# Preparing the first half of a recurrence inside a linear attention, moving the last scatters, and joining PSUM banks of two heads

## Chip, cores, metric

One core of a Trainium2 chip runs one program that computes eight layers, one after the other. The metric is device microseconds from start to end of one execution. Before the change the median of three runs is 2433.83 us (2418.57 to 2437.38).

## What is computed

The input is 4 batches of 1024 tokens with 128 features. Each of eight blocks is `x = layernorm(x + f(x))`. The first four (a gated recurrence, slots, a sparse attention, a two-way mixture) are not touched. What matters here are the blocks five to eight:

```python
# 5: linear attention, 16 heads of 64, causal, cos and sin weighted
S_cos += kc[:, None] * v[None, :];  S_sin += ks[:, None] * v[None, :]
num = qc @ S_cos + qs @ S_sin;  den = max(qc . z_cos + qs . z_sin, 1e-6)
out = (num / den) @ Wo + bo
# 6: eight experts, the two likeliest per token, silu(gate) * up
# 7: recurrence of 16 states for each of 256 channels
x  = resid * rsqrt(mean(resid^2) + eps) * norm_w
xs = silu(conv4(x @ in_w.T));  delta = softplus(xs @ wd1.T @ wd2.T + b)
h  = exp(delta * A) * h + (delta * xs) * B[t];  y = sum_n h_n * C[t]
y  = (y + xs * W_D) * silu(x @ skip_w.T) @ out_w.T;  return resid + y
# 8: eight experts, those within a probability mass of 0.8 per token
```

## The kernel before

Features are kept twice: `xN[b]` with tokens on the partitions and `xT[b]` with features on them, one pair per batch.

**Linear attention** (`l2_attn`, line 919 on). A quarter is 256 tokens of a batch (16 quarters), and a unit is a pair of heads in a quarter: 128 units. The loop over `t` runs a software pipeline: projection of unit `t + 2`, keys of `t + 1`, sums within the quarter (`l2_within`, line 1104) and from the states before (`l2_before`) of unit `t` into the PSUM tiles `po0` and `po1`, one bank for each head; scores and state sums of `t + 1`; then `l2_out` (line 1134) takes unit `t` out of PSUM. TensorE's order in this loop is as written (`manual_schedule`); the other engines are ordered by a scheduler at build time. `l2_out` issues four pairs: ScalarE scales 65 columns into `nsin` (L1142), VectorE multiplies 65 others and adds (`num`, L1145). PSUM is cut into two banks `pj` for projections, values and transposes, `po0`, `po1`, `pr`, and three shared with the experts.

Side work advances by one `yield` per unit: values of the next quarter (`l2_values`, line 1014: a tile `cv1` with a column of ones set by GpSimd at L1019, VectorE's add L1029, ScalarE's scaling L1036; two buffers), the output projection of a quarter, and, after the last quarter of a batch, `l2_dispatch` (line 1271). It ranks the eight experts for each token and scatters the batch's rows into `xrows` by 16 indirect DMAs on GpSimd (L1359), each made to wait for a recent projection (`beat`) so that they are spread out. As soon as the rows of a batch are there, the experts of block 6 (`l2_ffn`, line 1377, 23 units of 128 rows per batch) advance by one step per unit. A step loads the weights of one expert (`wx`, 384 KB on SP's queue, four buffers), and runs an expert unit on TensorE. `l2_combine` gathers a batch's results by 16 indirect DMAs on GpSimd (L1504), weighs and adds them and normalizes; it is a side generator that advances once per step. After it the batch is `done`.

**Recurrence** (`l3`, line 1549). It works in eight halves, 512 tokens each, two per batch. `l3_prepare` (line 1652) makes what a half needs: norm, transposes, projection `pxe`, a convolution of four taps on VectorE, tanh, the projections `pdb` and `pd`, softplus out of Abs, Exp and Ln, and the tiles `dl` (delta), `ud` (delta times input) and `rows` (B and C, stored to DRAM on SP's queue). `l3_scan` (line 1752) does 16 steps: SP loads a row of B and of C to all partitions (`bn`, `cn`, 256 KB each, four buffers), GpSimd multiplies `db = ud * bn` (L1782), ScalarE takes the exponential `da` (L1786), VectorE scans (L1787), GpSimd multiplies `hc = db * cn` (L1798), and TensorE adds up the 16 results in PSUM (`pys`). For the last three batches pairs of `hc` are added by a DMA first (L1802). Beside the scan of one half the next half is prepared, the one before is finished, the remaining steps of block 6 run (two per scan step in the first half, one in the others) and the experts of block 8 (`l3_experts`, `ph` and `py` with weights `wh`) take three or four steps per scan step. What is left of them runs after the last scan.

Before the first scan, `l3` runs block 6 until batch 0 is `done`, and then prepares half 0 with a step of block 6 at each `yield`. Since tile pools of the recurrence (`l3_pools`, line 1641) take the place of those of the linear attention, this starts when the linear attention ends.

Of the kernel before, what the change touches and what calls it, by code (L numbers as in the profile page):

```python
# [18 lines left out]
P = 128  # L19
# [39 lines left out]
class Net:  # L59
# [859 lines left out]
    def l2_attn(self, load, dispatch, moe):  # L919
# [7 lines left out]
        with ExitStack() as ctx:  # L927
# [9 lines left out]
            for t, n in dict(pj=2, po0=1, po1=1, pr=1).items():  # L937
                self.psq[t] = ctx.enter_context(
                    tc.tile_pool(name=f"ps_{t}", bufs=n, space=bass.MemoryType.PSUM)
                )  # L940
# [12 lines left out]
            side = []  # L953
# [9 lines left out]
            for t in range(-2, n + 4):  # L963
# [20 lines left out]
                if "put" in self.m2["st"][0] if t > 0 else False:  # L984
                    early(moe)
                if 0 <= t < n:
                    self.l2_out(units[t])
                    if t % NP2 == NP2 - 1:
                        Q = units[t]["Q"]
                        side.append(self.l2_project_out(Q))  # L990
                        if Q["c0"] + NQ == NC:
                            side[-1] = chain(side[-1], dispatch(Q["b"]))
# [3 lines left out]
            for g in side:  # L996
                for f in g:
                    pass
# [15 lines left out]
    def l2_values(self, Q):  # L1014
        nc, c2 = self.nc, self.c2
        wp = c2["wp"]
        for c in range(2):
            v1 = wp.tile([P, NH2, VW], F32, name="cv1")
# [85 lines left out]
    def l2_within(self, u):  # L1104
        Q, hp = u["Q"], u["hp"]
        u["po"] = [self.psb(f"po{i}", [P, 2, 2 * VW], f"po{i}") for i in range(2)]
        for i in range(2):
            for c in range(2):
                self.nc.tensor.matmul(  # L1109
                    out=u["po"][i][:, c, :],  # L1110
                    lhsT=u["a"][:, i, c, :],
                    rhs=Q["v"][c][:, 2 * hp + i, :, :].rearrange("p a d -> p (a d)"),
                    start=c == 0,
                    stop=False,
                    skip_group_check=True,
                )

    def l2_before(self, u):

        Q, hp = u["Q"], u["hp"]  # L1120
        for c in range(1 if Q["q"] == 0 else 0, 2):
            s = slice(c * P, (c + 1) * P)
            for i in range(2):
                h = self.HALF[i]
                self.nc.tensor.matmul(
                    out=u["po"][i][:, c, :],
# [7 lines left out]
    def l2_out(self, u):  # L1134
# [3 lines left out]
        for i in range(2):  # L1138
            for c in range(2):
                k = Q["c0"] + c  # L1140
                t = wp.tile([P, VW], F32, name="nsin", bufs=4)
                nc.scalar.activation(  # L1142
                    t, po[i][:, c, VW : 2 * VW], AF.Copy, scale=trig[:, k, 1:2]
                )
                nc.vector.scalar_tensor_tensor(  # L1145
                    num[:, c, i, :], po[i][:, c, 0:VW], trig[:, k, 0:1], t, ALU.mult, ALU.add
                )
# [123 lines left out]
    def l2_dispatch(self, b):  # L1271
# [84 lines left out]
        key, put = f"put{b}", []  # L1356
        for c in range(NC):
            for k in range(2):
# [10 lines left out]
                self.tc.add_to_no_dep_group(key, i)  # L1369

                self.tc.add_manual_dep(i, self.beat.name, SYNC, reason="spread out")
# [5 lines left out]
    def l2_ffn(self, wp):  # L1377
# [10 lines left out]
        for t in range(-8, n + 4):  # L1388
# [18 lines left out]
            for g in side[:]:  # L1407
                if next(g, self) is self:
                    side.remove(g)
# [124 lines left out]
    def l3_load(self):  # L1534
        return dict(
            wskip=self.load("s_in", [P, 2, E3]),
            we=self.load("s_e", [P, 2, ND + D]),
            wd2=self.load("s_d2", [DDELTA + 1, E3]),
            br=self.load_row("h_br", NE),
            wr=self.load("h_router", [P, NE]),  # L1540
            b2=self.load("h_b2", [NE, D]),
        )

    def load_row(self, name, n):
        t = self.const.tile([P, n], F32, name=f"sb_{name}")
        self.nc.sync.dma_start(out=t, in_=self.io[name].to_broadcast([P, n]))
        return t

    def l3(self, w3, moe, fp):

        nc, tc, c = self.nc, self.tc, self.const
# [8 lines left out]
        c3 = self.c3  # L1563
        neg1 = c.tile([P, 1], F32, name="neg1")
        nc.vector.memset(neg1, -1.0)
        c3.update(w3, aneg=aneg, cw=cw, neg1=neg1)
# [3 lines left out]
        while "done" not in self.m2["st"][0]:  # L1570
            next(moe)
        for f in self.l3_prepare(halves[0]):
            next(moe)
        work = self.l3_experts(fp)
        c3["todo"] = []
        end = iter(())
        for i, u in enumerate(halves):
# [6 lines left out]
            for f in self.l3_scan(u):  # L1584
                next(end, None)
                next(nxt, None)
                busy = next(moe, moe) is not moe
# [53 lines left out]
    def l3_pools(self, ctx):  # L1641
# [3 lines left out]
        dp = ctx.enter_context(  # L1645
            tc.tile_pool(name="ssmd", bufs=2, space=bass.MemoryType.DRAM)
        )
        banks = ctx.enter_context(self.banks(y0=1, y1=1, da=2, ff=4))
        self.mtags = dict(t="ff", h=("ff",), o="ff")
        self.c3 = dict(sp=sp, wp=wp, dp=dp, ctx=ctx, banks=banks)  # L1650

    def l3_prepare(self, u):

        nc, c3, b, h = self.nc, self.c3, u["b"], u["h"]
        sp, wp, dp = c3["sp"], c3["wp"], c3["dp"]
        wdb = c3["we"][:, :, 0:ND]

        sq = sp.tile([P, 4, D], F32, name="sq3", tag="s1")
        ms = wp.tile([P, 4], F32, name="ms3")
# [12 lines left out]
        pt = self.psb("ff", [P, 4, P], "pt")  # L1672
        for k in range(4):
            self.tr(pt[:, k, :], sq[:, k, :])
        xnT = wp.tile([P, 512], F32, name="xnT")
# [6 lines left out]
        tail = wp.tile([P, 2, K1], F32, name="tail") if h == 0 else u["prev"]["tail"]  # L1682
        u["tail"] = tail
        xs = wp.tile([P, 2, 512], F32, name="xs3")
        for ec in range(2):
            p = self.psb("ff", [P, 512], "pxe")
            self.mm(p, c3["wskip"][:, 1, ec * P : (ec + 1) * P], xnT)
            xc = sp.tile([P, 512], F32, name="xc", tag="s1")
# [28 lines left out]
        db = sp.tile([ND, 512], F32, name="db1", tag="s2")  # L1717
        rows = dp.tile([2 * NST, 512], F32, name="rows")
        p = self.psb("ff", [ND, 512], "pdb")
# [6 lines left out]
        dl = wp.tile([P, 2, 512], F32, name="dl")  # L1726
        ud = wp.tile([P, 2, 512], F32, name="ud")
        us = sp.tile([P, 2, 512], F32, name="sp_u")
        v = sp.tile([P, 2, 512], F32, name="sp_w")
        p2 = []  # L1730
        for ec in range(2):
            p2.append(self.psb("ff", [P, 512], f"pd{ec}"))
            self.mm(p2[ec], c3["wd2"][:, ec * P : (ec + 1) * P], db[0 : DDELTA + 1, :])
            nc.scalar.activation(us[:, ec, :], p2[ec], AF.Abs)
            nc.vector.tensor_single_scalar(dl[:, ec, :], p2[ec], 0.0, ALU.max)
        nc.scalar.activation(us, us, AF.Exp, scale=-1.0)
        nc.scalar.activation(v, us, AF.Identity, bias=self.ones[:, 0:1])

        for ec in range(2):
            nc.scalar.activation(p2[ec], v[:, ec, :], AF.Identity, bias=c3["neg1"])  # L1740
        nc.scalar.activation(v, v, AF.Ln)
        yield
        for ec in range(2):
            p = p2[ec]
            nc.vector.tensor_sub(p, us[:, ec, :], p)
            nc.vector.tensor_add(p, dl[:, ec, :], p)
            nc.vector.tensor_add(p, v[:, ec, :], p)
            nc.vector.tensor_mul(ud[:, ec, :], xs[:, ec, :], p)
            nc.scalar.copy(dl[:, ec, :], p)  # L1749
# [338 lines left out]
def program(tc, io):  # L2088
    with ExitStack() as ctx:
# [7 lines left out]
        )  # L2097
        with ExitStack() as ff:
            last = n.front(ff, w0, W, d, dp)
            keep = ctx.enter_context(tc.tile_pool(name="moek", bufs=1, side="right"))  # L2100
            mt = ctx.enter_context(tc.tile_pool(name="moet", bufs=2, side="right"))
# [4 lines left out]
        later = {}  # L2106

        def load():
            n.l2_ffn_load()
            later.update(n.l3_load())  # L2110
            n.l2_rows(keep, md, dp)

        moe = n.l2_ffn(mt)
        with w2:
            md = w2.enter_context(tc.tile_pool(name="moed", bufs=1, side="right"))
            n.l2_attn(load, n.l2_dispatch, moe)
        n.l3_pools(ctx)
        fp = ctx.enter_context(tc.tile_pool(name="top", bufs=2, side="right"))
        n.l3(later, moe, fp)
# [17 lines left out]
```

## Time and profile before

| What | us |
|---|---|
| median of 3 runs | 2433.83 |
| profiled execution | 2426.07 |
| its span, first to last instruction | 2424.3 |
| TensorE busy | 2077.0 (86%) |
| VectorE, ScalarE busy | 1439.7, 1335.6 |
| GpSimd busy | 860.8 |
| first and last `pqk` projection of the linear attention | 638.0, 1376.7 |
| last copy of attention output (`coT`) | 1399.3 |
| first and last `db` on GpSimd | 1476.8, 2261.4 |
| last `pys` | 2283.2 |
| end of last `h_acc` | 2416.9 |

Busy times are of one execution on the one core. TensorE's overlapping passes make its busy time an upper view of its work. A share over the whole span mixes stages with different limits, so the stages are read one by one. A line number is one of the kernel before; L127 is the helper that issues matmuls, so that those are told apart by the names of their tiles.

### The profile page before, as it was taken

Reading aid. Unit: us, or ns where it says so; the run is one execution under the profiler, and the core shown is the slowest. Engines: PE = TensorE matmul, PEld = TensorE weight load, DVE = VectorE, ACT = ScalarE, POOL = GpSimd, SP = SyncE. Lnnn points to the kernel's source line nnn. Section 1 sums busy time; section 2 is a strip of 40 time slices with the busy share of each in tenths; the row PEclk is TensorE's granted clock in tenths of the full one; section 3 lists DMA queues with packets and bytes.
Section 4 is the critical chain, followed back from the end, with each engine's and each line's share of the span. In section 5 each row is a group of like instructions: output and inputs, shape, how many; then the busy total and the mean of one; then the engine's idle time right before and its main releaser. Section 6 shows DMA issues by size and latency. Waiting matters only on the chain. (4 is left out here: it accounts for less than half of the span.)

```text
span 2424.3 us, 35395 instructions
## 1 busy us (share of the span) xinstructions
PE 2077.0 (86%) x12170; PEld 1456.7 (60%) x12170; DVE 1439.7 (59%) x4207; ACT 1335.6 (55%) x2934; POOL 860.8 (36%) x557
## 2 busy tenths in 40 slices
PE   6767979979899999999989865776788989798988
PEld 3455655544577777787768754553455656465666
DVE  6457733433466666755656556676778777676431
ACT  6543433332456565656655555657677776666443
POOL 5001220000000011001021137868899979688500
PEclk9657969989999999999989988997999989898999
DMA  3000110013000010021222156663577766575421
GB/s 101 0 18 21 29 33 7 12 64 92 1 1 1 1 33 22 16 76 41 62 74 82 42 158 190 210 181 91 147 187 185 201 165 184 149 205 151 113 66 48
DMA packets 138517, 209.87 MB, mean 87 GB/s; under 512 B 18598, under 2 KB 75937, under 8 KB 138081
## 3 DMA queue, kind: packets, MB, share of 16 engines
q1 hardware_dynamic: 126048, 172.82, 24.0%
q0 software_dynamic: 12288, 34.79, 6.8%
q8 instruction: 96, 1.57, 0.3%
q14 instruction: 85, 0.69, 0.1%
HBM read 159.24 MB, written 23.16 MB: 75 GB/s over the span
## 5 line engine op out<-in xcount | busy, mean ns | idle before, releaser
L1798 POOL TENSOR_TENSOR hc<-db,cn 128x1024 f32<-128x1024 f32 x128 | 317.2, 2501 | 81.1 <-PE pys L127 29.7
L1782 POOL TENSOR_TENSOR db<-ud,bn 128x1024 f32<-128x1024 f32 x128 | 326.0, 2574 | 44.1 <-ACT dl L1749 16.4
L127 PEld LDWEIGHTS py<-wh,hh 128*128 128x128 f32 x2048 | 249.5, 193 | 78.2 <-issue 43.7
L127 PE MATMUL ph<-xT,wh 128*128 128x512 f32 x512 | 262.7, 632 | 24.8 <-DVE h_acc L1926 7.5
L1145 DVE SCALAR_TENSOR_TENSOR num<-po,sb_c_trig,nsin 128x65 f32<-128x65 f32 x512 | 132.7, 279 | 232.1 <-ACT nsin L1142 218.3
L127 PE MATMUL py<-wh,hh 128*128 128x128 f32 x2048 | 255.9, 277 | 13.0 <-ACT hh L1910 12.7
L1910 ACT ACTIVATE hh<-ph,sb_cols 128x512 f32<-128x512 f32 x256 | 171.1, 681 | 137.7 <-PE ph L127 111.5
L1142 ACT ACTIVATE nsin<-po,sb_c_trig 128x65 f32<-128x65 f32 x512 | 148.3, 316 | 176.7 <-DVE num L1145 103.5
L1786 ACT ACTIVATE da<-dl,aneg 128x512 f32<-128x512 f32 x256 | 175.4, 689 | 74.6 <-DVE db L1787 72.8
L1019 POOL MEMSET cv<- 128x16 f32 x32 | 4.0, 127 | 497.7 <-ACT cv L1036 354.8
L127 PE MATMUL pys<-hc,sb_c_ident 128*128 128x512 f32 x320 | 164.3, 642 | 14.7 <-DMA hc<-hc 14.7
L127 PEld LDWEIGHTS ph<-xT,wh 128*128 128x128 f32 x512 | 92.6, 201 | 117.5 <-issue 63.9
L1926 DVE SCALAR_TENSOR_TENSOR h_acc<-py,gt,h_acc 128x128 f32<-128x128 f32 x256 | 71.9, 343 | 153.0 <-PE py L127 145.3
L1787 DVE TENSOR_TENSOR_SCAN db<-da,carry,db 128x512 f32<-128x512 f32 x128 | 156.8, 1266 | 5.9 <-ACT da L1786 4.3
L1787 DVE TENSOR_TENSOR_SCAN db<-da,db 128x512 f32<-128x512 f32 x128 | 149.8, 1206 | 11.3 <-ACT da L1786 10.1
L127 PE MATMUL pqk<-xT,wE 128*128 128x256 f32 x512 | 137.0, 391 | 7.4 <-DVE cv L1029 6.0
L1359 POOL DMA_INDIRECT xrows<-xN,di x64 | 61.9, 968 | 221.2 <-ACT kN L1063 216.4
L1109 PE MATMUL po<-cv,a 128*128 128x130 f32 x1024 | 136.9, 276 | 0.9 <-DVE num L1145 0.9
L1109 PEld LDWEIGHTS po<-cv,a 128*128 128x128 f32 x1024 | 125.5, 192 | 2.6 <-issue 1.0
L1036 ACT ACTIVATE cv<-cv,sb_c_trig 128x520 f32<-128x520 f32 x128 | 86.4, 724 | 51.4 <-DVE cv L1029 46.0
L127 PEld LDWEIGHTS pys<-hc,sb_c_ident 128*128 128x128 f32 x320 | 61.1, 203 | 80.4 <-issue 59.1
L127 PEld LDWEIGHTS pqk<-xT,wE 128*128 128x128 f32 x512 | 87.9, 191 | 25.3 <-DVE cv L1029 10.1
(430 smaller groups left out, 4440.4 us busy)
## 6 DMA issues: line engine op xcount, KB each, us to landing
wx<-in_wF SPq DMA_DIRECT2D x92, 384.0 KB
wh<-in_wH SPq DMA_DIRECT2D x64, 512.0 KB
bn<-rows SPq DMA_DIRECT2D x128, 256.0 KB
cn<-rows SPq DMA_DIRECT2D x128, 256.0 KB
hc<-hc POOLq DMA_DIRECT2D x48, 512.0 KB
xrows<-zero SPq DMA_DIRECT2D x4, 1472.0 KB
xg<-xrows SPq DMA_DIRECT2D x20, 256.0 KB
yrows<-ys SPq DMA_DIRECT2D x20, 256.0 KB
```

The costliest lines, as they stand in the source:

```text
L127: return self.nc.tensor.matmul(out=out, lhsT=lhsT, rhs=rhs, start=start, stop=stop)
L1036: nc.scalar.activation(Q["v"][c][:, hs, i, :], v1[:, hs, :], AF.Copy, scale=c2["trig"][:, k, i : i + 1],)
L1109: self.nc.tensor.matmul(out=u["po"][i][:, c, :], lhsT=u["a"][:, i, c, :], rhs=Q["v"][c][:, 2 * hp + i, :, :].rearrange("p a d -> p (a d)") ...
L1142: nc.scalar.activation(t, po[i][:, c, VW : 2 * VW], AF.Copy, scale=trig[:, k, 1:2])
L1145: nc.vector.scalar_tensor_tensor(num[:, c, i, :], po[i][:, c, 0:VW], trig[:, k, 0:1], t, ALU.mult, ALU.add)
L1359: i = nc.gpsimd.indirect_dma_start(out=rows[:, :], out_offset=bass.IndirectOffsetOnAxis(ap=st["dest"][k][:, c : c + 1], axis=0), in_=self. ...
L1782: nc.gpsimd.tensor_mul(db, ud, bc[0])
L1786: nc.scalar.activation(da, dl[:, ec, :], AF.Exp, scale=aneg[:, j : j + 1])
L1787: nc.vector.tensor_tensor_scan(db[:, ec, :], da, db[:, ec, :], carry[:, ec, n : n + 1] if h else 0.0, ALU.mult, ALU.add,)
L1798: nc.gpsimd.tensor_mul(hc, db, bc[1])
L1910: nc.scalar.activation(ht, ph, AF.Relu, bias=self.col("h_b1", i=e * NK + k))
L1926: nc.vector.scalar_tensor_tensor(acc[:, c, :], py[:, c, :], gt[:, c, e : e + 1], acc[:, c, :], ALU.mult, ALU.add,)
```

## The change

- Half 0 of the recurrence is prepared inside the linear attention. When batch 0 is `done`, one step of `l3_prepare` follows each unit. It has no room of its own: its tiles stand in `xT[0]`, `xT[1]` and `xT[2]`, the features of batches whose linear attention is over, and a small pool `first`; its PSUM tiles come out of the two `pj` banks. Softplus is done for one block of 128 channels after the other there, with a bank for each. The weights and constants of the recurrence are loaded with those of block 6.
- The 16 scatters of the last batch are left over by `l2_attn` (the generator stops at `yield "put"`) and are issued one per step of the first scan, without the wait for a beat.
- Side generators of block 6 advance twice per step.
- `po0` and `po1` become one tile of two banks, and `l2_out` issues two pairs of instructions with 130 columns, each over both heads, in place of four with 65.
- The value tile `cv1` has one buffer in place of two, and `nsin` two in place of four.

```diff
-            for t, n in dict(pj=2, po0=1, po1=1, pr=1).items():
+            for t, n in dict(pj=2, po=1, pr=1).items():
...
                 if "put" in self.m2["st"][0] if t > 0 else False:
                     early(moe)
+                    if "done" in self.m2["st"][0]:
+
+                        if begin is None:
+                            begin = self.l3_prepare(self.l3_early(first))
+                        next(begin, None)
...
-            for g in side:
+            for g in (begin, *side):
                 for f in g:
-                    pass
+                    if f == "put":
+                        self.m2["rest"] = g
+                        break
...
-            v1 = wp.tile([P, NH2, VW], F32, name="cv1")
+            v1 = wp.tile([P, NH2, VW], F32, name="cv1", bufs=1)
...
-        u["po"] = [self.psb(f"po{i}", [P, 2, 2 * VW], f"po{i}") for i in range(2)]
+        po = self.psq["po"].tile([P, 2, 512], F32, name="po")
+        u["po"] = po[:, :, 0 : 4 * VW].rearrange("p i (c d) -> p i c d", c=2)
...
-        for i in range(2):
-            for c in range(2):
-                k = Q["c0"] + c
-                t = wp.tile([P, VW], F32, name="nsin", bufs=4)
-                nc.scalar.activation(
-                    t, po[i][:, c, VW : 2 * VW], AF.Copy, scale=trig[:, k, 1:2]
-                )
-                nc.vector.scalar_tensor_tensor(
-                    num[:, c, i, :], po[i][:, c, 0:VW], trig[:, k, 0:1], t, ALU.mult, ALU.add
-                )
+        for c in range(2):
+            k = Q["c0"] + c
+            t = wp.tile([P, 2, VW], F32, name="nsin")
+            nc.scalar.activation(t, po[:, :, c, VW : 2 * VW], AF.Copy, scale=trig[:, k, 1:2])
+            nc.vector.scalar_tensor_tensor(
+                num[:, c], po[:, :, c, 0:VW], trig[:, k, 0:1], t, ALU.mult, ALU.add
+            )
...
         key, put = f"put{b}", []
+        yield "put"
...
-                self.tc.add_manual_dep(i, self.beat.name, SYNC, reason="spread out")
+                if b < B - 1:
+
+                    self.tc.add_manual_dep(i, self.beat.name, SYNC, reason="spread out")
...
-            for g in side[:]:
-                if next(g, self) is self:
+            for g in side * 2:
+                if next(g, self) is self and g in side:
                     side.remove(g)
...
-        while "done" not in self.m2["st"][0]:
-            next(moe)
-        for f in self.l3_prepare(halves[0]):
-            next(moe)
+        halves[0] = dict(self.c3["first"], **{k: halves[0][k] for k in ("prev",)})
...
             for f in self.l3_scan(u):
                 next(end, None)
                 next(nxt, None)
+                for k in range(1):
+                    next(self.m2["rest"], None)
                 busy = next(moe, moe) is not moe
...
+    def l3_early(self, pool):
+        half = lambda b, i: self.xT[b][:, i * 512 : (i + 1) * 512]
+        k = [0]
+        def at(name, shape):
+            if name in ("xnT", "tail", "xs3"):
+                return pool.tile(shape, F32, name=name)
+            if name in ("dl", "ud"):
+                return self.xT[1 if name == "dl" else 2].rearrange("p (e t) -> p e t", e=2)
+            if name == "sq3":
+                return half(2, 0).rearrange("p (k d) -> p k d", d=D)
+            if name == "db1":
+                return half(2, 1)[0:ND]
+            if name == "xc":
+                k[0] += 1
+                return half(0, k[0] % 2)
+            return half(0, name == "sp_w")[:, None, :]
+        u = dict(b=0, h=0, at=at, ff=self.bank("pj"))
+        self.c3["first"] = u
+        return u
...
+        for g in ((0,), (1,)) if "at" in u else ((0, 1),):
+            us, v = at("sp_u", [P, len(g), 512]), at("sp_w", [P, len(g), 512])
...
+            if g[-1] == 0:
+                yield
```

## The prediction, on record before the result

> **What bounds the kernel now.** I read the table of stages (busy time per engine in stretches of 60 us) first, because the program is a row of stages with different limits; then GpSimd's instructions in order of time at the weakest stretch, then the waits inside the linear attention, then the costliest groups.
>
> In the stages the columns are the stretch, its length, busy us (instructions) of PE, PEld, DVE, ACT, POOL, the granted PE clock, DMA share, GB/s:
>
> ```profile
> 1320.00:1380.00 60.00, 56.29 (x515) 47.25 (x512) 35.95 (x147) 35.68 (x105) 10.57 (x11) 1.00 0.14 42
> 1380.00:1440.00 60.00, 42.94 (x306) 37.52 (x306) 35.90 (x132) 29.35 (x84) 8.43 (x9) 0.91 0.45 131
> 1440.00:1500.00 60.00, 31.81 (x148) 22.50 (x148) 30.27 (x68) 35.12 (x77) 41.63 (x33) 0.72 0.64 192
> 1500.00:1560.00 60.00, 45.10 (x219) 30.42 (x220) 49.07 (x79) 43.19 (x99) 51.52 (x25) 0.94 0.66 201
> 1620.00:1680.00 60.00, 35.99 (x107) 18.93 (x108) 46.16 (x84) 43.28 (x81) 47.49 (x27) 0.77 0.36 107
> 1740.00:1800.00 60.00, 51.60 (x225) 31.82 (x225) 43.14 (x91) 42.67 (x84) 52.01 (x26) 0.94 0.69 180
> ```
>
> Until 1402 us PE is full (717 of 762 us from 640 to 1402). From 1440 to 1500 no engine reaches 42 of 60 us. From 1500 on GpSimd carries the recurrence (52 of 60). After 2283 PE alone is full again (125 of 141), with the experts that are left. GpSimd in the weak stretch, as start, us, operation, [idle before it <- who ended it]:
>
> ```profile
> 1374.66 0.96 POOL L1359 DMA_INDIRECT xrows<-xN,di  x1 [3.47 <-ACT kN L1063]
> 1423.36 0.99 POOL L1504 DMA_INDIRECT yg<-yrows,di  x1 [47.74 <-DMA xg<-xrows]
> ...
> 1468.18 0.96 POOL L1359 DMA_INDIRECT xrows<-xN,di  x1 [0.30 <-issue]
> 1476.77 2.36 POOL L1782 TENSOR_TENSOR db<-ud,bn 128x1024 f32<-128x1024 f32 x1 [7.63 <-PE py L127]
> ```
>
> The last line is the first product of the first of eight halves of the recurrence. It can't come earlier, since the half is prepared (norm, convolution, softplus) only after the linear attention ends, and behind 16 gathers and 16 scatters on GpSimd's own queue. Inside the linear attention:
>
> ```profile
> PE pa_m L127 <- DVE a L1098: 8.3, 11, 1.5
> PE kp_mo L131 <- DVE state L1085: 7.5, 18, 1.9
> PE pqk L127 <- DVE cv L1029: 6.0, 12, 0.6
> PE kp_mo L127 <- DVE state L1085: 5.8, 4, 2.3
> ...
> ACT nsin L1142 <- DVE num L1145: 102.4, 223, 1.4
> ```
>
> PE waits little there (about 33 us in all) and 29 us of that for VectorE. ACT and DVE hand the `po` banks to each other (102 us, 223 times) without PE noticing. The two groups that the change joins, and GpSimd's two products:
>
> ```profile
> L1145 DVE SCALAR_TENSOR_TENSOR num<-po,sb_c_trig,nsin 128x65 f32<-128x65 f32 x512 | 132.7, 279 | 232.1 <-ACT nsin L1142 218.3
> L1142 ACT ACTIVATE nsin<-po,sb_c_trig 128x65 f32<-128x65 f32 x512 | 148.3, 316 | 176.7 <-DVE num L1145 103.5
> L1798 POOL TENSOR_TENSOR hc<-db,cn 128x1024 f32<-128x1024 f32 x128 | 317.2, 2501 | 81.1 <-PE pys L127 29.7
> L1782 POOL TENSOR_TENSOR db<-ud,bn 128x1024 f32<-128x1024 f32 x128 | 326.0, 2574 | 44.1 <-ACT dl L1749 16.4
> ```
>
> **The change, part by part.** Matmul counts stay; the order of each queue in the built program tells what moves.
>
> *Joined banks.* 512 + 512 instructions of 65 columns become 256 + 256 of 130. A 128-wide copy with a scale takes 0.39 us on ACT (`yg`), a 128-wide multiply-add from PSUM 0.34 on DVE (`h_acc`), so ACT goes from 148 to 256 x 0.39 = 100 us, DVE from 133 to 87. PE is full, so these 48 and 46 us are room, not time. What PE can win is the 29 us that it waits for DVE: between 0 and -29; I take -10, as these waits also hang on other DVE work. One instruction now reads both banks, so ACT and DVE alternate strictly. Today one unit's chain runs from 1370.83 to about 1373.1 (2.3 us); four alternating steps of 0.39 and 0.34 with gaps of 0.1 make 1.9, and PE waited only 0.9 us for it in the whole stage.
>
> [...]
>
> *Early preparation.* Its PE work is 6 matmuls of 512 columns in two passes of 0.43 us (4 passes of `ph` take 1.72 in the chain of waits), 5.2 us, and four transposes, 0.6: +5.8 us on a full PE. DVE gets about 15 us more and ACT about 20 with table loads (1.28 each), within some ten units of 5.8 us at the end. Both have the room on average, but not in each unit: one channel block of the convolution is 3.7 us of DVE work (0.79 + 3 x 0.74 and three short ones) put ahead of the next `num` and `a`, on which PE waits. Its PSUM tiles also hold one of the two `pj` banks, through which projections, values and transposes then pass singly. Bounds 0 and 35 us (all exposed); I take 12, about 1.2 per unit. The value tile with one buffer I put at 0, since its pieces are a unit (5.8 us) apart and the scaling that frees it takes 2 x 0.72; without that cover see rival C. So the linear attention gets -10 + 6 + 12 = 8 us longer (bounds -23 and +41).
>
> *Start of the recurrence.* The loads of its rows (`bn`) stand on SP's queue behind six expert weight loads, which wait for PE. In the list of SP's issues the sixth after 1377 is through at 1401. Landing: a `cn` issued about 1495 let GpSimd go at 1499, so 4 us. 1401 + 4 + 8 = 1413 instead of 1476.8: -64 us.
>
> *What the gap held moves into the first two halves.* Today GpSimd works 64 products of 2.35 us and 32 gathers of 1.25 (0.95 + 0.30 between) from 1476.8 to 1706.9: 190 of 230 us, 83%. Afterwards 16 scatters and 16 gathers more stand between the products, less 16 gathers that move to the third half: 48 x 1.25 + 150 = 210. No faster than 210; at today's share 254; at the share of the second half alone (95 of 132, 72%) 292. I take 250, nearest to the row of the same two halves: +20. The last scatters no longer wait for a beat; they stand before products of the first half, and the loads of its rows stand on SP behind the last scatter, ahead of `bn` 15. Four buffers of `bn` cover that.
>
> *Expert layer work left over.* At the 60th of 160 pairs of summing matmuls, the new order has 86 narrow matmuls (32 passes take 3.57 in the chain, so 0.22 each) and five wide ones (0.86) less behind it, 19 + 4 = 23 us of PE. At the 100th pair both orders have done the same (83 against 84 `ph`). Today that stretch runs from 1704 to 1935, PE busy 203 of 231, so 28 us are free. If half of the 23 finds a gap it costs +12 (bounds 0 and +23). 16 gathers (20 us) fall into the same stretch, where GpSimd has 208 of 231: beside, not on top. Rest from 1935 to 2424: unchanged order, 0. Table loads 107 to 106: 0. Side work advanced twice per step, and the constants made at load time: 0, as gathers and scalings sit on GpSimd and ACT with room (74 of 762 us and 454 of 762 until 1402).
>
> [...] The clock here was 0.70 from 1402 to 1477 and 0.84 from 1402 to 1704. [...]
>
> **Sum.** -64 + 20 + 12 = -32 against the profiled execution (2426.1; span 2424.3 and 1.8 around it): 2394. The four executions shown average 2429, 3 more than the profiled, so 2397 for a typical run; the median shown is 2434.
>
> **Rivals.**
> B, the start moves but the first two halves give it back: GpSimd at 74% as in today's second half, 210/0.74 = 284, ending at 1697 against 1707; less 12: about 2428. For it: the second half already stands (14 us for one DVE scan at 1600), and finish, preparation, combine and experts meet there. Against: the first half, with gathers too, ran at 97%.
> D, GpSimd keeps 95% in both: 221, end at 1634, 73 - 12 = 61: 2368.
> C, slower: the value tile's one buffer. Filling it (memset 0.13, DVE add 0.69, two ACT scalings of 0.72) takes 2.3 us; if PE sees all of it at each of 31 hand-overs, 71 us: 2468. From 1.0 us per hand-over (32/31) on the gain is gone. For it: PE already waits 6.0 us for `cv`, the memset shares GpSimd's queue with gathers that wait for stores (25.9 us once), and ACT runs in order. Against: the hand-overs lie a unit apart.
> That the preparation isn't early at all is excluded: in the program's order the first `da` stands on ACT before the last transposes of the linear attention.
>
> **Numbers.** Forecast (2380 to 2412) 0.47, D 0.12, B 0.26, C 0.15. Range 2360 to 2445: it takes in B and the start of C and leaves out most of C and the better part of D. One per cent (24 us on 2434) is about what a measurement of this kernel can tell from no change. Faster by more: D and nearly all of the forecast, 0.57; within: B and the forecast's edge, 0.28; slower: C, 0.15.
>
> **What would show it.** First `db` at 1405 to 1420 (start step); end of the linear attention 1395 to 1420, with PE's waits for `a`, `state`, `cv` below 29 us; POOL's second half ending near 1663; equal time from the 100th pair to the end (489 us). I am wrong if the attention grows by over 20 us, or if GpSimd's first two halves last over 280.

## The result, and the profile after

The changed kernel takes 2420.57 us (median of 20 runs, 2409.3 to 2432.4), the kernel before 2427.82 (20 runs, 2414.24 to 2437.38). The ratio is 0.9968, 95% interval [0.9955, 0.9981]: 7 us faster, inside the 1% that the prediction called no change, where it had forecast 32 us less. The profiled execution took 2412.3 us against 2424.3.

The kernel before took 2392 to 2427 us in the groups of runs below, each on one chip (on chip 12 once 2392 and once 2424), so ratios to it within a group are compared. Beside two of the experiments the changed kernel was run again: 1.001 [0.9993, 1.0026] and 0.9974 [0.9953, 0.9995].

The stages after, in the columns of the prediction:

```profile
1380.00:1440.00 60.00, 37.56 (x276) 33.27 (x276) 44.11 (x92) 36.56 (x85) 21.30 (x9) 0.85 0.55 175
1440.00:1500.00 60.00, 40.67 (x161) 26.49 (x162) 38.81 (x91) 29.23 (x74) 48.43 (x39) 0.78 0.53 163
1500.00:1560.00 60.00, 36.91 (x113) 19.71 (x113) 43.43 (x61) 34.39 (x65) 49.67 (x24) 0.73 0.47 148
1740.00:1800.00 60.00, 55.69 (x295) 40.49 (x296) 47.87 (x78) 34.31 (x65) 48.64 (x25) 0.92 0.74 205
```

The weak stretch at 1440 is gone from GpSimd (48 of 60 us), but TensorE does no more there than 37 to 41 us, and from 1740 on it is fuller than before (55.7 against 51.6). GpSimd's first product in order of time:

```profile
1378.10 0.96 POOL L1366 DMA_INDIRECT xrows<-xN,di  x1 [3.71 <-ACT kN L1070]
1411.59 2.34 POOL L1823 TENSOR_TENSOR db<-xT,bn 128x1024 f32<-128x1024 f32 x1 [32.54 <-DVE rt_l L1211]
```

It stands at 1411.6, where the prediction had 1413. TensorE's waits inside the linear attention, and the joined groups:

```profile
PE pqk L127 <- DVE cv L1036: 13.4, 14, 4.2
PE pa_m L127 <- DVE a L1105: 12.5, 26, 2.2
PE kp_mo L131 <- DVE state L1092: 7.0, 16, 1.9
```

```profile
L1151 DVE SCALAR_TENSOR_TENSOR num<-po,sb_c_trig,nsin 128x130 f32<-128x130 f32 x256 | 89.2, 348 | 268.5 <-ACT nsin L1150 251.2
L1150 ACT ACTIVATE nsin<-po,sb_c_trig 128x130 f32<-128x130 f32 x256 | 94.8, 370 | 131.7 <-PE po L1134 72.3
```

The joined instructions take 89 and 95 us, as estimated (87 and 100). Where the time went is seen when the span is cut at the same places of both programs: the last projection, and the first product of half 1, of half 3 and of half 5, which are GpSimd's 1st, 33rd and 65th `db`. First the kernel before (end of attention to half 1, halves 1 and 2, halves 3 and 4), then the changed one:

```profile
1376.70:1476.80 100.10, 61.23 (x384) 50.07 (x383) 48.73 (x173) 49.83 (x129) 30.59 (x33) 0.78 0.49 145
1476.80:1699.60 222.80, 162.71 (x764) 108.91 (x764) 156.86 (x279) 141.05 (x308) 175.13 (x95) 0.89 0.56 167
1699.60:1883.40 183.80, 154.96 (x693) 94.17 (x692) 145.34 (x265) 132.10 (x234) 161.43 (x80) 0.95 0.67 177
```

```profile
1376.30:1411.60 35.30, 30.13 (x249) 27.15 (x247) 20.96 (x69) 29.39 (x68) 0.97 (x2) 0.95 0.38 106
1411.60:1647.50 235.90, 154.95 (x623) 98.81 (x624) 171.52 (x297) 130.65 (x277) 191.63 (x111) 0.80 0.55 170
1647.50:1869.40 221.90, 188.97 (x915) 126.22 (x915) 167.66 (x305) 146.27 (x292) 176.59 (x95) 0.92 0.63 178
```

The gap is 64.8 us shorter, halves 1 and 2 take 13 us more, halves 3 and 4 take 38 us more. Behind half 5 both take the same (540.9 and 542.9). In halves 3 and 4 TensorE's work is 34 us more (155 to 189). It comes from ahead: from the last projection to half 3 TensorE works 223.9 of 322.9 us before and 185.1 of 271.2 after, 0.69 and 0.68 of the time. The change cut 52 us out of a stretch in which TensorE still worked, 39 us of its work were put off, and 34 us of it came in halves 3 and 4, where it is busy 0.85 of the time: 34/0.85 = 40 us, about what they grew by. Some 26 us of it are 15 units of block 6 (120 matmuls `ph` from `xgT` in halves 3 and 4, none before). Which part of the change put them there is seen in e8 and e16 below.

In halves 1 and 2 TensorE is busy less than before (0.66 of the time against 0.73). One reason is seen in VectorE's instructions. The ranking of the last batch's experts (L1211 to L1360) now runs beside GpSimd's products. VectorE in the changed kernel:

```profile
1424.30 2.73 DVE L1229 TENSOR_TENSOR rt_g<-rt_p 128x512 f32<-128x512 f32 x1
1426.96 2.84 DVE L1230 TENSOR_TENSOR rt_q<-rt_p 128x512 f32<-128x512 f32 x1
1429.84 2.71 DVE L1231 TENSOR_TENSOR rt_q<-rt_q,sb_c_jle 128x512 f32<-128x512 f32 x1
1438.39 2.17 DVE L1287 TENSOR_SCALAR sel<-rt_r 128x64 f32<-128x64 f32 x1
1449.34 2.33 DVE L1828 TENSOR_TENSOR_SCAN db<-da,db 128x512 f32<-128x512 f32 x2
1452.92 6.87 DVE L1273 TENSOR_TENSOR tend<-nt 128x7 f32<-128x7 f32 x1
```

GpSimd at the same times, and the TensorE instruction behind `sel`:

```profile
1424.14 2.35 POOL L1839 TENSOR_TENSOR hc<-db,cn 128x1024 f32<-128x1024 f32 x1
1426.44 5.56 POOL L1823 TENSOR_TENSOR db<-xT,bn 128x1024 f32<-128x1024 f32 x2
1450.47 2.37 POOL L1839 TENSOR_TENSOR hc<-db,cn 128x1024 f32<-128x1024 f32 x1
1452.78 2.37 POOL L1823 TENSOR_TENSOR db<-xT,bn 128x1024 f32<-128x1024 f32 x1
1455.12 4.64 POOL L1839 TENSOR_TENSOR hc<-db,cn 128x1024 f32<-128x1024 f32 x2
```

```profile
1440.61 0.69 PE L127 MATMUL ppos<-sel,sb_c_stri 128*128 128x64 f32 x2 [11.25 <-DVE sel L1287]
```

The same instructions of VectorE in the kernel before, where they lay in the gap:

```profile
1415.19 0.69 DVE L1223 TENSOR_TENSOR rt_g<-rt_p 128x512 f32<-128x512 f32 x1
1422.95 0.19 DVE L1281 TENSOR_SCALAR sel<-rt_r 128x64 f32<-128x64 f32 x1
1431.80 0.16 DVE L1267 TENSOR_TENSOR tend<-nt 128x7 f32<-128x7 f32 x1
```

A sum of 7 elements takes 6.87 us in place of 0.16 and ends at 1459.79, when the four products that began at 1450.47 end (1459.76). `rt_g` and the two `rt_q` wait for one product each: `rt_g` ends at 1427.03, just behind the product that ended at 1426.49, and the next two products take 5.56 us in place of 4.64. The scan at 1449.34, whose `da` is in PSUM, is not held up: the two take 2.33 us, and the median of one is 1.21 over all of these scans. TensorE waits 11.25 us for `sel`. The instructions shown that stand still have two operands in SBUF, or, as `sel` (2.17 us in place of 0.19), compare from SBUF to SBUF; why they stand still no run here shows. The sum at 1452.92 waits for the three products that are left of a row of four. What decides between one and three is open.

### The profile page after: what moved, and what is told of

It reads as the page before. It is cut to its first block, busy times and chain, and to the rows that moved or that the text cites. A ratio compares the mean times of both kernels' runs of the same rounds, so it can differ in the third digit from the quotient of the medians.

```text
span 2412.3 us, 34775 instructions
## 1 busy us (share of the span) xinstructions
PE 2068.1 (86%) x12170; PEld 1454.9 (60%) x12170; DVE 1420.2 (59%) x3949; ACT 1287.5 (53%) x2679; POOL 863.0 (36%) x557
## 4 chain that ended last, share of the span: by engine, by line
PE 60%; DVE 18%; ACT 10%; issue 7%; DMA 2%; POOL 1%; another core or an unknown queue 1%; SPq 0%; ACTq 0%; POOLq 0%; DVEq 0%
PE ph L127 12%; PE py L127 8%; PE po L1118 4%; PE pqk L127 4%; PE po L127 4%; PE pt L131 4%; PE pa_m L127 3%; DVE db L1828 3%; PE pys L127 3%; PE po L1134 3%; PE kp_mo L127 3%; PE pv L127 2%; PE pr L127 2%; DVE a L1105 1%; PE kp_mo L131 1%
## 5 line engine op out<-in xcount | busy, mean ns | idle before, releaser
L1823 POOL TENSOR_TENSOR db<-ud,bn 128x1024 f32<-128x1024 f32 x112 | 287.1, 2638 | 29.3 <-DVE pmv L159 23.2
L1151 DVE SCALAR_TENSOR_TENSOR num<-po,sb_c_trig,nsin 128x130 f32<-128x130 f32 x256 | 89.2, 348 | 268.5 <-ACT nsin L1150 251.2
L1827 ACT ACTIVATE da<-dl,aneg 128x512 f32<-128x512 f32 x224 | 153.3, 689 | 66.7 <-DVE db L1828 63.2
L1150 ACT ACTIVATE nsin<-po,sb_c_trig 128x130 f32<-128x130 f32 x256 | 94.8, 370 | 131.7 <-PE po L1134 72.3
```

The costliest lines, as they stand in the source:

```text
L1150: nc.scalar.activation(t, po[:, :, c, VW : 2 * VW], AF.Copy, scale=trig[:, k, 1:2])
L1151: nc.vector.scalar_tensor_tensor(num[:, c], po[:, :, c, 0:VW], trig[:, k, 0:1], t, ALU.mult, ALU.add)
L1823: nc.gpsimd.tensor_mul(db, ud, bc[0])
L1827: nc.scalar.activation(da, dl[:, ec, :], AF.Exp, scale=aneg[:, j : j + 1])
```

## The experiments

The table has, for each kernel, the ratio to the kernel before on its chip and, from its one profile, the us between the places cut as above, with TensorE's idle time from the last projection to the end. TensorE's work there is 856 to 868 us in each of them, except 841 (e1), 846 (e2) and 851 (e9).

| Kernel | ratio [95%] | to half 1 | halves 1, 2 | halves 3, 4 | idle |
|---|---|---|---|---|---|
| before | 1 | 100 | 223 | 184 | 184 |
| after | 0.9968 [0.9955, 0.9981] | 35 | 236 | 222 | 174 |
| e1, after, 15 units out | 0.9940 [0.9916, 0.9964] | 37 | 235 | 214 | 178 |
| e2, before, 15 units out | 0.9958 [0.9939, 0.9977] | 90 | 208 | 181 | 180 |
| e3, after, more steps | 1.0051 [1.0030, 1.0072] | 36 | 249 | 212 | 181 |
| e4, before, joined banks | 0.9964 [0.9947, 0.9981] | 89 | 215 | 187 | 165 |
| e5, after again | 1.0010 [0.9993, 1.0026] | 38 | 234 | 219 | 174 |
| e6, after, no indirect DMAs | 0.9942 [0.9920, 0.9963] | 37 | 224 | 216 | 159 |
| e7, before, no indirect DMAs | 0.9894 [0.9871, 0.9918] | 80 | 188 | 193 | 143 |
| e8, after, not early | 0.9956 [0.9938, 0.9974] | 89 | 182 | 212 | 165 |
| e9, after, no ranking | 0.9890 [0.9848, 0.9931] | 39 | 211 | 218 | 159 |
| e10, not early, no ranking | 0.9943 [0.9921, 0.9966] | 81 | 184 | 220 | 163 |
| e11, after, ranked first | 1.0028 [1.0002, 1.0054] | 85 | 205 | 231 | 191 |
| e12, after, 12 units ahead | 0.9942 [0.9920, 0.9965] | 38 | 235 | 215 | 165 |
| e13, after, ranking in PSUM | 0.9930 [0.9906, 0.9954] | 37 | 228 | 212 | 170 |
| e14, e13 and e12 | 1.0006 [0.9986, 1.0027] | 40 | 237 | 224 | 187 |
| e15, after again | 0.9974 [0.9953, 0.9995] | 37 | 238 | 224 | 181 |
| e16, after, scatters back | 1.0003 [0.9987, 1.0018] | 35 | 250 | 215 | 179 |
| e17, e13, ranks in PSUM too | 0.9902 [0.9882, 0.9922] | 36 | 227 | 213 | 162 |
| e18, e17, not early | 1.0002 [0.9986, 1.0017] | 99 | 186 | 220 | 186 |

The numbers of the theories begin anew with each group of runs. The expectations give 127 us for half 1 of the changed kernel, 219 for halves 1 and 2 and 231 to 234 for halves 3 and 4; cut at the products named above, its three profiles have 132 to 136, 234 to 238 and 219 to 224.

**The expert units.** e1 and e2 have the same edit:

```diff
-            if 0 <= t < n:
+            late = lambda u: u["st"]["b"] == B - 1 and u["j"] >= 8
+            if 0 <= t < n and not late(units[t]):
                 self.l2_hidden(units[t], wp)
```

> The changed kernel, leaving out TensorE's, ScalarE's and VectorE's work of the last 15 expert units of block 6 (batch 4, units 9 to 23; their weight loads, the stores of the result rows, with rows of an earlier group, and the gathers stay). These are the units that the changed order leaves for halves 3 and 4 of the recurrence (1631 to 1865 us, 234 us against 179 before). Theory 1 (the left-over units are not hidden there: TensorE's queue is 86 to 88 % busy in both kernels): halves 3 and 4 together fall to about 195 us and the whole to 2375 to 2390. Theory 2 (the loss there is GpSimd's, by the 16 gathers of 1.25 us and what waits for them): nearly nothing moves, 2410 to 2420. Theory 3 (the loss is a transfer, the rows or weights being late): nothing moves, since all loads stay.

> The kernel before, leaving out the same work of the same 15 expert units. There they run between 1402 and 1704 us, where TensorE is idle for 100 of 302 us. Theory 1: they were hidden there, so the time falls by 0 to 12 us, to 2416 to 2428, a third or less of what the changed kernel gains by the same edit. If work of TensorE costs its own length wherever it stands, both fall by the same 25 to 40.

Halves 3 and 4 fall to 214 us, 6 to 10 less than in the changed kernel, where theory 1 had 195. From the last projection to the end e1 takes 1019 us, and the changed kernel 1030 to 1038 in its three profiles, for 15 to 21 us less of TensorE's work (841 against 856 to 862): the units cost most of their length, half of it behind half 5, as experts of block 8 move up. As all loads stay, this part is not a transfer's. In e2 halves 1 and 2 fall from 223 to 208 us. But e1 is 0.3 to 0.7% under the changed kernel and e2 0.4% under the kernel before, so the units' own work does not tell the two apart.

```diff
-                if i == 0:
-                    for k in range(1):
+                if i < 2:
+                    for k in range(2 - i):
                         next(moe, None)
```

> The changed kernel with three steps of block 6 per scan step in the first half (two before) and two in the second (one before), so that no unit is left for halves 3 and 4. Theory 1: halves 3 and 4 shorten by 30 to 45 us to about 195, halves 1 and 2 (240 us, TensorE idle for 80 of them) lengthen by 5 to 25, the whole is 2385 to 2410. Theory 2: the 16 gathers only move into half 2, where GpSimd has less room, 2412 to 2430. Against both: if the units wait for the last scatters (done at 1502 us) the first half stalls by more than 25 and the whole is above 2425.

Halves 3 and 4 shorten by 8 to 12 us, where theory 1 had 30 to 45, and halves 1 and 2 lengthen by 10 to 15, as it had. The whole, 2406 us, is in its range only because the times on this chip were lower: the kernel before took 2395. From half 5 on it takes 548 us (539 in e5), and TensorE waits 34 us there at the head of block 8 (`pgt`, `pb`; 9 in e5). Work that is done sooner meets the next thing that is not there yet.

**The joined banks alone** (the `po` part of the diff, on the kernel before).

> The kernel before with the joined banks alone (one tile of two banks for two heads, two pairs of instructions with 130 columns in place of four with 65). Prediction: the linear attention 10 us shorter (bounds 0 and 29), which the recurrence gets in full: 2415 to 2420. Rival (joining frees ScalarE and VectorE, on which TensorE hardly waits): 0 to 3 us, 2425 to 2428. Other rival (strict alternation of the two engines holds the tile longer): the attention 5 to 15 us longer, 2433 to 2443.

0.9964 is 9 us on 2395, about the prediction's figure. The attention (first to last projection) takes 732.9 us; without the joined banks it takes 735.9 on the same chip (e2) and 738.7 in the first profile, so 3 to 6 us of the 9 are gained there. This part alone is worth as much as the whole change.

**GpSimd's indirect DMAs, and the early preparation.**

```diff
-            for k in range(2):
+            for k in range(0 if b in (1, 2, 3) else 2):
                 i = 4 * h + c
                 nc.gpsimd.indirect_dma_start(
```

> The changed kernel as it is, beside the three others, since chips differ by over 1 % in their absolute times: 0.995 to 0.998 of the time before, and the same places in its profile as in the first one (first db 35 us after the last pqk, halves 1 and 2 of the recurrence 219 us, halves 3 and 4 234 us, to 8 us).

> The changed kernel, leaving out the 64 indirect DMAs of GpSimd that stand among the products of the first four halves: the gathers of batches 2, 3 and 4 (their weighting reads the batch's features instead) and the scatters of the last batch (its rows stay zero). All of TensorE's, VectorE's and ScalarE's work stays. Theory 1 (GpSimd paces the first four halves, and every indirect DMA that stands there costs its own 1.25 us and more): halves 1 to 4, 453 us in the first profile, shorten by 60 to 95 us, and the whole by 50 to 90 against the changed kernel. Theory 2 (the first four halves are paced by TensorE's queue, 340 of 453 us busy and in order): they shorten by less than 25.

> The kernel before with the same 64 left out. There 32 of them lie in the gap before the first product, where GpSimd idled 44 of 75 us, and 32 among the products. Theory 1: halves 1 to 4 (398 us) shorten by 35 to 50, the gap by 0 to 20; the whole by 35 to 60, and the changed kernel, without indirect DMAs in both, leads by 20 to 45 us in place of the measured 8. Theory 2: less than 20, and the changed kernel's lead stays under 15.

Without the 64 DMAs the changed kernel gains 15 us and the kernel before 26, so the changed one is 14 us behind, where theory 1 had it 20 to 45 ahead. These DMAs cost time in both, but they do not explain where the early start went.

```diff
-                    if "done" in self.m2["st"][0]:
...
-                        next(begin, None)
...
+        while "done" not in self.m2["st"][0]:
+            next(moe)
+        for f in self.l3_prepare(halves[0]):
+            next(moe)
```

> The changed kernel with the early preparation undone: half 0 is prepared after the linear attention as before, with a step of block 6 at each part; the joined banks, the moved scatters, the one value tile and the side work advanced twice stay. Theory 1 (the early start is worth its 64 us less what is moved behind it): first db 50 to 65 us later, halves 1 to 4 shorter by 30 to 50, the attention 5 to 10 shorter; the whole within 12 us of the changed kernel. Rival (the early preparation gains by itself, and another part of the change takes it back): 20 to 50 us slower than the changed kernel. Other rival (it costs more than it gains): over 12 us faster than the changed kernel.

Undoing the early preparation makes the kernel 14 us faster than e5 on the same chip, the last of the three cases, if only just; by the ratios of the two other measurements of the changed kernel it is 3 to 4 us. The attention is 10.6 us shorter (733.5 against 744.1), half 1 begins 51 us later after it, halves 1 and 2 take 52 us less (182 against 234). So in e5 the first two halves give the whole early start back.

Halves 3 and 4 take 212 us in e8, 7 less than in e5, but 28 more than in the kernel before. The 15 units stand there in e8 too (120 matmuls), so it is not the early preparation that puts them there; with the last scatters issued earlier (e16, below) 3 units are left.

**The ranking.** Theory 3 is the standstill, theory 4 a fixed account of TensorE's work.

```diff
+        if b == B - 1:
+            last = m2["st"][b - 1]
+            st["eti"], st["dest"], st["wts"] = last["eti"], last["dest"], last["wts"]
+            yield
+        else:
...
+            if u["b"] == 0 and h == 0 and n == 0:
+                self.tc.add_manual_dep(i, self.m2["ranked"].name, SYNC, reason="ranks first")
...
+        for k in range(12):
+            next(moe)
         end = iter(())
```

The first five lines are e9 and e10, the next two e11, the last e12.

> The changed kernel, leaving out the ranking of the last batch (its router and some 40 small VectorE instructions; it uses the ranks and weights of the batch before, the scatters, units and gathers stay). Theory 3 (the ranking is what the early start collides with: VectorE's two-input instructions on SBUF stand still while GpSimd multiplies, 128x7 took 7.68 us in place of 0.16, and TensorE waited 11.2 + 5.7 us behind them in half 1): half 1 falls from 127 to 95 to 108 us, TensorE's idle time in halves 1 to 4 from 114 to 85 to 100, and the whole to 0.985 to 0.995 of the time before. Theory 4 (TensorE's work after the attention, 862 us in every kernel so far, is what sets the time, and idle time removed at one place comes back at another): half 1 shortens and the rest lengthens; the whole stays at 0.996 to 1.001.

> The same left out of the changed kernel without early preparation (0.9956 of the time before), where the ranking runs in the gap at 0.2 us an instruction. Theory 3: the gap shortens by 0 to 8 us, the whole by no more, 0.992 to 0.996. Theory 4: the same.

> The changed kernel, in which the first product of the recurrence waits for the last instruction of the last batch's ranking; nothing is left out. Theory 3: the first db is 12 to 28 us later (at about 1415 to 1428 where the control had 1400), half 1 shorter by 20 to 35, the whole equal or up to 12 us shorter than the changed kernel. If the ranking does not matter there (theory 1 or 2): half 1 keeps its 127 us, and the whole is 12 to 28 us longer.

> The changed kernel with 12 units of block 6 put ahead of the first scan step, as the gap did before; half 0 is still prepared in the attention. Theory 4: the first db is 25 to 45 us later, but the units are gone from halves 3 and 4, TensorE's idle time after the attention stays at 165 to 178 us, and the whole is within 8 us of the changed kernel. If the start of the recurrence sets the end, as the prediction had it, the whole is 15 to 30 us longer.

Without the ranking half 1 falls to 104.9 us and TensorE's idle time in halves 1 to 4 to 94 (114 to 120 in the changed kernel), and the changed kernel gains 0.8 to 1.2%, 19 us or more; without early preparation the same edit gains 0.1%. That is theory 3, and theory 4 falls here. Of a start 42 us earlier than in e10, halves 1 and 2 of e9 give back 27, where e5 gave back all. In e11 half 1 falls to 101 us, as theory 3 had it, but units and gathers have moved ahead of it too; the first product is 48 us later, not 12 to 28, and the whole is slower. It also shows how little the start is worth: 48 us later cost 4 to 15 us, by the three ratios of the changed kernel. In e12 the first product is not later at all, as GpSimd does not wait for units, and as many units as in the changed kernel stand in halves 3 and 4 (120 matmuls); the gain, 6 to 8 us beside the first measurement and e15, is within theory 4's 8, but it does not come from moved units.

**The standstill alone.** In e13 each two-input instruction of the ranking has one operand in PSUM; e17 keeps the ranks there too. Nothing is left out.

```diff
-        q = tile("q", NE, NE)
+        q = ps([P, n, NE, NE], "rt_q") if free else tile("q", NE, NE)
...
-        off = wp.tile([P, NC, NE], F32, name="off")
+        off = new([NC, NE], "off")
...
-        rank = tile("r", NE)
+        rank = bank[:, :, 2 * NE :] if free else tile("r", NE)
```

> The changed kernel with the ranking of the last batch written so that no VectorE instruction of it has two operands in SBUF (one of the two is put into a PSUM bank, some 12 copies of 0.2 us more); nothing is left out. Theory 3 (these instructions stand still while GpSimd multiplies, and TensorE behind them): none of the ranking's instructions takes over 1 us where the control had 2.7, 2.85, 2.74, 2.2 and 7.68; TensorE's wait for sel in half 1 falls from 11 us to under 6; half 1 falls from 127 to 104 to 118 us, and the whole by 8 to 25 us against the changed kernel on the same chip. If leaving the ranking out gained by its own length and not by the standstill: under 5 us.

> The same with 12 units of block 6 ahead of the first scan step, which alone was 0.9942 of the time before. Theory 3 and theory 4 together: the two edits act on different waits of TensorE, so the whole is 10 to 30 us under the changed kernel on the same chip, and a version that is faster than both kernels. If time removed at one place comes back at another: no faster than the better of the two edits alone.

> The changed kernel once more, as the companion of these runs on their chip: 0.995 to 1.002 of the time before (0.9968 and 1.001 so far).

> The changed kernel with the last batch's 16 scatters issued with the rest of the linear attention's side work, ahead of the first scan step, still without a beat; early preparation and joined banks stay. Theory 4 (units of the last batch come late because their rows do): the units are done earlier, halves 3 and 4 shorter by 20 to 40 us than the control's 231, the first db or half 1 later by 10 to 25; the whole 0 to 15 us under the changed kernel. Rival (the moved scatters are what let the recurrence start early): first db 15 to 25 us later and the whole 10 to 25 us longer.

e13 is 11 us faster than e15 on its chip. One instruction in it still stood still, a comparison from SBUF to SBUF with one input; VectorE and GpSimd in e13:

```profile
1443.28 6.59 DVE L1299 TENSOR_SCALAR sel<-rt_r 128x64 f32<-128x64 f32 x1
```

```profile
1440.52 4.70 POOL L1854 TENSOR_TENSOR db<-xT,bn 128x1024 f32<-128x1024 f32 x2
1445.18 2.34 POOL L1870 TENSOR_TENSOR hc<-db,cn 128x1024 f32<-128x1024 f32 x1
1447.48 2.34 POOL L1854 TENSOR_TENSOR db<-xT,bn 128x1024 f32<-128x1024 f32 x1
```

It ends with the last product in the row (1449.8). Half 1 fell from 135.8 us in e15 only to 124.1, short of the 104 to 118 expected; halves 3 and 4 are 12 us shorter (212 against 224), but from half 5 on 13 us are lost again (552 against 539). The two edits together (e14) lose what each gains alone; why is open. With the scatters back (e16) the first product is not later, against the rival; 3 of the 15 units are left in halves 3 and 4, which shorten by 9 us only, and halves 1 and 2 lengthen by 12, against theory 4, so that the whole is 6 us behind e15.

> The version with the ranking's operands in PSUM, where also the ranks themselves stay in PSUM: the one instruction of the ranking that still stood still in it was the comparison sel (128x64 from SBUF to SBUF, 6.59 us in place of 0.2), and TensorE waited 6.3 us for it. Theory 3: sel takes under 0.5 us, TensorE's wait for it under 3 us, half 1 falls from 124 to 112 to 120 us, and the whole from 0.993 of the time before to 0.988 to 0.992, the level of the kernel that leaves the ranking out (0.989). If the standstill of sel only shifts another wait: 0.992 to 0.995.

> The same without early preparation, to see what the early preparation is worth once the ranking does not collide with it. Theory 3: the ranking runs in the gap, where nothing stands still, so the edit changes nothing, 0.993 to 0.996 of the time before, as without the edit (0.9956); the early preparation is then worth 5 to 15 us. If the edit helps by other means than the standstill: 0.985 to 0.992.

VectorE and GpSimd in e17:

```profile
1424.48 0.66 DVE L1234 TENSOR_TENSOR rt_g<-rt_p,prl 128x512 f32<-128x512 f32 x1
1431.84 0.21 DVE L1299 TENSOR_SCALAR sel<-prl 128x64 f32<-128x64 f32 x1
```

```profile
1424.46 2.38 POOL L1861 TENSOR_TENSOR db<-xT,bn 128x1024 f32<-128x1024 f32 x1
1429.10 4.68 POOL L1861 TENSOR_TENSOR db<-xT,bn 128x1024 f32<-128x1024 f32 x2
```

With an operand in PSUM, `rt_g` takes 0.66 us and `sel` 0.21 while GpSimd multiplies; half 1 takes 120.8 us. The whole is 0.9902, as expected: 2400.42 us against 2423.87, and by the ratios faster than the changed kernel too (0.9968 to 1.0010). Without early preparation the same edit is 1.0002, 0.5% above e8, which theory 3 did not expect: its gap has one wait of 18.7 us of TensorE for an expert unit, whose cause I did not find. Changes of that size without a known cause, here and in e14, may be part of the other ratios too. What speaks for the standstill in e13 and e17 is that the instructions no longer stand still and that half 1 is 11 to 15 us shorter. The early preparation is worth 23 us beside e18, and about 13 beside e8 (0.9956); in the changed kernel it cost 3 to 14. In e17 halves 1 and 2 give back 40 of the 62 us of earlier start.

## Why the prediction was wrong, step by step

- *Joined banks, -10:* right for the whole (e4: 9 us), though only 3 to 6 of it lie in the attention.
- *Early preparation, +18 in the attention:* it cost 10.6 us (e5 against e8) and 11.0 (e17 against e18). The attention's total of +8 was measured at +6.5 (738.7 to 745.2). TensorE's wait for `cv` rose by 7.4 us and that for `a` by 4.2; rival C's 2.3 us at each hand-over did not come.
- *Start, 1413:* 1411.6, but partly by luck. The part ahead of the attention, the same in both programs, took 6.9 us less in this execution; from the last projection the start took 35.3 us, where the sum had 28.
- *First two halves, +20:* right. To their last product they took 242.9 us against 230.1 (+12.8), and to the 60th pair of summing matmuls, where the next term begins, +18.9. By the prediction's count GpSimd did 210 of 243 us of work there, 86%, where it had assumed 84% (210 of 250).
- *"If half of the 23 finds a gap it costs +12 (bounds 0 and +23)":* this step failed. Its stretch, from the 60th to the 100th pair, took 265.2 us in place of 230.1, so it cost +35. First before, then after:

```profile
1704.40:1934.50 230.10, 201.98 (x937) 126.26 (x936) 177.26 (x324) 165.65 (x294) 207.46 (x101) 0.96 0.68 178
1658.10:1923.30 265.20, 227.97 (x1121) 151.73 (x1120) 199.66 (x377) 176.37 (x342) 216.23 (x114) 0.94 0.64 179
```

  The count of the work was right: TensorE had 26 us more to do, for 23. None of it found a gap: TensorE's idle time in the stretch did not fall but rose, from 28 to 37 us. So the bound was wrong too, as it took 28 idle us of 231 for room, and the idle time grew with the work. The term does not hang on the early start either: without it (e8) the stretch takes 267.7 us, and without the 15 units (e1) 249.1. Why it does not fall to 230 in e1 is open.
- *Rest, 0:* right, 489.8 and 489.0 us from the 100th pair on.

With the measured terms the sum is -65.2 (start) + 18.9 + 35.1 - 0.8 = -12.0, the difference of the two spans. Rival B, that the start is given back in the first two halves, came nearest to the time (2428). As it was put, it did not happen: it had them take 284 us with GpSimd at 74%, and they took 243 at 86%. But beside e8 they do give the whole start back: there, without an early start, they take only 182 us, with 15 units and 16 gathers in halves 3 and 4 as in the changed kernel. Beside the kernel before, that gain hides the loss. The granted clock fell to 0.80 in halves 1 and 2 (0.89 before), and TensorE still idled there for 81 us.

What no step had: the ranking of the last batch was moved from a gap without products to a place beside them. Mending a part of its standstill gained 11 us (e13 beside e15), and with the rest mended (e17) the kernel is 0.7% under the first measurement of the changed kernel, 16 us, with nothing left out. What stays open is why e14 loses both gains, and the 18.7 us wait in e18.

## What to carry to other kernels

Before an early start is counted as gained, see how busy the bounding engine is in the stretch that is cut out: here 39 us of TensorE's work were put off, not saved, and its idle time in the stretch where that work came, 28 of 230 us, was not room for it: it became 37 of 265. Test the parts of a change one by one: here the first two halves gave the early start back, and moved scatters put units into the next two. List every small instruction that the move brings beside GpSimd's products, and try one operand in PSUM for those of VectorE that read two SBUF operands or that compare from SBUF to SBUF.

## What the runs showed of the hardware

VectorE's instructions of the ranking with two SBUF operands, and a one-input comparison from SBUF to SBUF, stood still beside GpSimd's products: 0.16 us became 6.87 (`tend` in the changed kernel), 0.19 became 6.59 (`sel` in e13), 0.69 became 2.7 to 2.8 (`rt_g` and `rt_q` in the changed kernel). With an operand in PSUM `rt_g` took 0.66 and `sel` 0.21 (e17). In the changed kernel a copy of one column (0.15 us at 1452.85) and a reduction (0.20 at 1451.59), from SBUF to SBUF beside the same products, did not stand still. Some went on when one product had ended, two only when the rest of a row of four products without a gap had (9.3 us for the row), and TensorE waited 11.25 us for `sel` in the changed kernel.
